# Four small reorderings in a float32 expert-mixture kernel on one core

## The chip, the cores and the metric

The kernel runs on one core of one Trainium2 chip. The metric is device time in microseconds (us). The kernel before was run three times: median 451.2 us, from 451.02 to 451.33. A profile was taken of one further execution, which took 450.84 us.

## The reference

Eight sequences of 512 tokens of width 256 attend to 64 prototypes each. The result, with the normalized token and an anchor vector, goes through a router, three experts and a gate. All in float32:

```python
nx = _layer_norm(x, ln_gamma, ln_beta)
q = nx @ Wq; k = prototype_bank @ Wk; v = prototype_bank @ Wv
weights = jax.nn.softmax(jnp.einsum('bth,bph->btp', q, k) * H ** (-0.5), axis=-1)
evidence = jnp.einsum('btp,bph->bth', weights, v)
combined = jnp.concatenate([nx, evidence, anchor], axis=-1)
router_probs = jax.nn.softmax(combined @ router_W + router_b, axis=-1)
h = jax.nn.silu(jnp.einsum('btc,ecr->bter', combined, e_w1) + e_b1)
expert_out = jnp.einsum('bter,erh->bteh', h, e_w2) + e_b2
routed = jnp.sum(expert_out * router_probs[..., None], axis=-2)
g = jax.nn.sigmoid(jax.nn.silu(combined @ gate_w1 + gate_b1) @ gate_w2 + gate_b2)
return x + g * (routed @ out_w + out_b)
```

## The kernel before

**Work.** The sequences go through in four pairs, `j` = 0 to 3; the text calls them pair 0 to pair 3, and pair 3 the last pair. Hidden dimensions lie on the 128 partitions, tokens along the free axis, 512 to a PSUM bank. The two sequences of a pair are treated as the two columns of a 2 by 2 block matrix, so that block products can be saved at the price of sums and differences of blocks, which VectorE and GpSimd make.

**Each pair has two parts.** In the first the gate's and the experts' first layers are multiplied (`gate_first`, `gate_layer`, and `expert_layer` in pair 0 or `half_layers` in the others; there the matmuls are of 64 rows, and two of them run side by side). In the second, `outputs`, come the gate's second layer and the experts' second layer, whose weights w2 have been multiplied by `out_w` beforehand. In pair 0 these are seven products of six matmuls each, with the points P1 to P7 between them; in the other pairs `twenty_products` does them as twenty block products, numbered 1 to 20.

**Twenty products.** The 512-token blocks of the pair are cut into blocks of 342 columns, `at[k, n]`. Each product is a `chain` of three matmuls, one for each expert, which appear as six records in the trace, since a float32 matmul is recorded as two. From product 19 on, the chains add in turn into two banks, Y and X. After a chain `read` lets VectorE add the bank's content to an accumulator in SBUF (`racc`), and the next chain into the same bank has to wait for that reading. Between them, differences (`less`) and sums (`plus`) of blocks of 128 x 1026 elements are made for later chains. After each chain stands a named point, c1 to c20, at which `run` calls steps of the next pair: the scores, the softmax, the transposes of its weights (`turn_weights`, parts 0, 1 and 2), the router's logits.

**Order.** The order on every engine is written out by hand: an engine issues its instructions in the order in which the code calls them, and waits at each for the semaphores of what it reads or overwrites. Which step stands at which point is set by the `put(between, point, step, ...)` lines at the end.

**What the change touches.** Four places:

- `second_layer` (line 550) multiplies w2 by `out_w` in pair 0, for one expert at a time. VectorE has transposed w2 in two halves, `k` = 0 and 1 (`transpose_second`, L548). Each bank holds two results of 256 columns, `d` = 0 and 1, and each is the sum of two matmuls, one for each `k`.
- `turn_weights`, parts 0 and 1, in pairs 1 and 2: one transpose of 128 x 512 (L850) and one of 32 x 256 (L854) on VectorE, called at point c13, ahead of product 13.
- The difference (0,1) = u - (2,0) in the last pair, called between product 16 and product 18. Product 10 multiplies it, and a sum on GpSimd reads it.
- `router_exp` of pair 1 on ScalarE, called at P3 of pair 0, ahead of `gate_first` of pair 1. `gate_first` multiplies into bank U, and a ScalarE copy (`keep_part`, L1206) saves what stands there before `gate_layer`'s product 6 is added to it.

Of the kernel before, what the change touches and what calls it, by code (L numbers as in the profile page):

```python
# [16 lines left out]
def kernel(  # L17
# [56 lines left out]
    KH = H // P  # L74
# [33 lines left out]
    def misc(name):  # L108
        spare.append(spare.pop(0))
        return bank(spare[-1], name)  # L110
# [439 lines left out]
    def second_layer(e):  # L550
        w2T = w2["T"]
        for i in range(0, RC, 2):
            ps = misc(f"ps_w2o_{e}_{i}")
            for d in range(2):
                for k in range(KH):
                    nc.tensor.matmul(  # L556
                        ps[:, d * H : (d + 1) * H], w2T[:, k, (i + d) * P : (i + d + 1) * P], ow_sb[:, k, :],
                        start=(k == 0), stop=(k == KH - 1),
                    )
            c = e * RC + i  # L560
            nc.scalar.copy(w2o[:, c : c + 2, :].rearrange("p c n -> p (c n)"), ps)
# [697 lines left out]
    def gate_first(j):  # L1259
        n = 0  # L1260
        gate_tile(j, 0, 0)
        U[n] = bank(0, f"ps_u_{j}_{n}")
        nx_product(j, n, 1, True)
        keep_part(n, 0, 0, U[n])
# [343 lines left out]
    def zero_ends(j):  # L1608
        nc.gpsimd.memset(hall[:, :, 2 * T :], 0.0)
# [13 lines left out]
    def twenty_products(j, run, gated, finish, store, last_gate):  # L1623

        last = j + 1 == NP
        V_, G = nc.vector, nc.gpsimd
# [3 lines left out]
        def less(engine, dst, p, m):  # L1630
            engine.tensor_tensor(at[dst], at[p], at[m], ALU.subtract)  # L1631

        def plus(engine, dst, p, m):
            engine.tensor_tensor(at[dst], at[p], at[m], ALU.add)  # L1634
# [71 lines left out]
            less(V_, "w", (2, 1), "u")  # L1706
        read("Y", 1, 1, ALU.subtract)
        nc.scalar.mul(at[2, 1], at[2, 0], -1.0)
        if not last:
            plus(V_, (3, 1), (0, 0), (3, 2))  # L1710
        run("c9")
        chain(20, (0, 2), 5, "X")
# [9 lines left out]
        chain(16, "w", "Y")  # L1722
        read("Y", 1, 2, ALU.subtract)
        if last:
            less(V_, (0, 1), "u", (2, 0))
            plus(G, (0, 2), (1, 0), (0, 1))
            less(G, (0, 2), (3, 0), (0, 2))
        run("c11")
# [279 lines left out]
    with tc.manual_schedule(engines=None):  # L2008
# [63 lines left out]
        for j in range(NP):  # L2072


            within, between = {}, {}

            def put(where, n, step, *args):
                where.setdefault(n, []).append(lambda: step(*args))

            if j == 0:  # L2080
                for e, points in enumerate(("AB", "SABCDE", "ACDE")):
                    for point in points:
                        put(within, (e, point), values_together, e, point)
                put(within, "gate first", value_weights, 0, 0, nc.scalar.copy, False)
                put(within, "gate early", value_differences, 0, 0)
                put(within, "gate early", value_weights, 0, 1, nc.scalar.copy, False)
                put(within, "gate", load_table, AF.Silu)
                put(within, (0, "S"), combine_x, 0, nc.vector, (3,))
                put(within, (0, "S"), value_differences, 0, 1)
                put(within, (0, "S"), router_part, 0)  # L2090
                put(within, (0, "A"), router_part, 1)
                put(within, (0, "A"), load_x, 2)
                put(within, (0, "A"), load_x, 3)
                put(within, (0, "B"), combine_weights, 1)
                put(within, (0, "B"), combine_weights, 2)
                put(within, (0, "B"), combine_gate)
                put(within, (0, "A"), router_logits, 0)
                put(within, (0, "A"), load_second, 1)
                put(within, (0, "C"), transpose_second, 0)
                put(within, (0, "C"), value_weights, 0, 2)  # L2100
                put(within, (0, "sums"), late_rows)
                put(within, (2, "W"), second_bias)
                put(within, (0, "C"), router_exp, 0)
                put(within, (0, "D"), router, 0)
                put(within, (0, "C"), load_second, 2)
                put(within, (0, "D"), second_layer, 0)
                put(within, (0, "D"), spread_probabilities, 0)
                put(within, (0, "D"), combine_second, 0)
                put(within, (1, "A"), transpose_second, 1)
                put(within, (1, "B"), second_layer, 1)  # L2110
                put(within, (1, "B"), combine_second, 1)
                put(within, (1, "C"), transpose_second, 2)
                put(within, (1, "C"), anchor_columns, 2)
                put(within, (1, "D"), second_layer, 2)
                put(within, (1, "D"), combine_second, 2)
                put(within, (1, "D"), values_together, 1, "D late")
            if j > 1:
                put(within, "gate early", router_exp, j)
                put(within, "gate early", lambda: later.pop()())
            if j == 0:  # L2120
                put(within, (2, "A"), gate_differences, 0)
            if j + 1 < NP:
                b0, b1 = 2 * j + 2, 2 * j + 3
                if j == 0:
                    put(between, "P7", load_x, b0 + 2)
                    put(between, "P7", load_x, b1 + 2)
                elif j + 2 < NP:
                    put(between, "f01", place_last_x, b1 + 2)
                if j == 0:
                    put(between, "P6", load_x_blocks, 0)  # L2130
                    put(between, "P6", load_x_blocks, 1)
                    for b in (b0, b1):
                        put(within, (0, "D"), statistics, b, 0, NT)
                    for b in (b0, b1):
                        put(within, (1, "S"), deviation, b)
                    for b in (b0, b1):
                        put(within, (1, "S"), normalize, b)
                        put(within, (1, "S"), store_x, b)
                    put(within, (1, "C"), regroup_x, b0)
                    put(within, (1, "B"), router_part, b0)  # L2140
                    put(within, (1, "B"), router_part, b1)
                put(between, "begin", transpose_blocks, b0)
                put(between, "gate", regroup_x, b1)
                put(between, "gate values" if j else "begin", value_weights, j + 1, E)
                put(between, "c2" if j else "begin", store_router_rows, j + 1)
                put(between, "c10" if j else "begin", spread_router_rows, j + 1)
                put(between, "c4" if j else "P5", transpose_blocks, b1)
                if j == NP - 3:
                    put(between, "c4", place_last_x, b0 + 2)
                put(between, "c9" if j else "P2 half", scores, j + 1)  # L2150
                if j:
                    for point, ts in (("p13", (0, 1)), ("c10", (2, 3))):
                        put(between, point, combine_x, j + 1, nc.gpsimd, ts)
                else:
                    put(between, "P2 half", combine_x, 1, nc.gpsimd)
                put(between, "c12" if j else "P7", softmax, j + 1)
                if j:
                    put(between, "c13", turn_weights, j + 1, (0, 1))
                    put(between, "c15", turn_weights, j + 1, (2,))
                    for e, point in enumerate(("c17", "c18")):  # L2160
                        put(between, point, router_logits, j + 1, (e,))
                    put(between, "c4", value_differences, j + 1, 0)
                else:
                    put(between, "P7", turn_weights, 1)
                    put(between, "P7", router_logits, 1)
                    put(between, "P7", value_differences, 1, 0)
                if not j:
                    put(between, "P3", router_exp, 1)
            if j == 0:
                for point in ("begin", "P1", "P6", "P2 half", "P2"):  # L2170
                    put(between, point, values_together, E, point)
            if not j:
                gate_first(j)
            gate_layer(j, within)
            if j:
                zero_ends(j)
                half_layers(j)
            else:
                for e in range(E):
                    expert_layer(j, e, within)  # L2180
            outputs(j, between)
# [34 lines left out]
```

## Time and profile before

| | before |
|---|---|
| median of three runs | 451.2 us (451.02 to 451.33) |
| the profiled execution | 450.84 us |
| its span, first to last instruction | 448.7 us |
| TensorE busy | 443.3 us, 99% |
| VectorE busy | 364.7 us, 81% |
| ScalarE busy | 229.4 us, 51% |
| GpSimd busy | 170.4 us, 38% |
| TensorE clock granted | 0.999 of full speed |

A line of a timeline tells when a run of like instructions began on one engine, how long it lasted, the source line, the operation, the tiles (written <- read) with buffer numbers left out, partitions x elements, how many there were, and in brackets how long the engine was idle before and what ended that. PE is TensorE, PEld its weight loads, DVE is VectorE, ACT is ScalarE, POOL is GpSimd. L1139 is the line of the helper that issues nearly all matmuls, so matmuls are told apart by their tiles. L1646 is the reading of a bank, L1631 a block difference (`less`), L1634 a block sum (`plus`). The ends of matmuls are modelled, and the bars of successive matmuls overlap.

### The profile page before, as it was taken

What the parts mean: (1) busy time and instruction counts of PE and PEld (TensorE: products, weight loads), DVE (VectorE), ACT (ScalarE), POOL (GpSimd) and SP (SyncE); (2) the same over time, 40 slices, a digit from 0 to 9 for tenths busy, and PEclk for the clock granted to TensorE, in tenths of its full rate; (3) what the DMA queues carried; (4) which work ended last, traced back from release to release, by engine and by line L of the source; (5) the groups of instructions that cost most, each with busy time, mean ns of one, the idle gap of its engine ahead of it and who ended that gap; (6) DMA issues with size and microseconds to landing.
All of it is one profiled execution on the core that took longest, in us unless ns stands there. A gap on an engine that the chain in (4) does not pass through costs nothing.

```text
span 448.7 us, 5750 instructions
## 1 busy us (share of the span) xinstructions
PE 443.3 (99%) x1807; PEld 231.7 (52%) x1807; DVE 364.7 (81%) x686; ACT 229.4 (51%) x417; POOL 170.4 (38%) x219
## 2 busy tenths in 40 slices
PE   8999999999999999999999999999999999999996
PEld 7644656444444444444666444445666444445665
DVE  3988889667969999879886989879867846689975
ACT  3545685548323257768533187668251265766000
POOL 6567767531242156109648320000465500001270
PEclk9999999999999999999999999999999999999999
DMA  8998699565741589979973294710561392000715
GB/s 251 380 188 197 108 266 166 99 106 110 76 66 23 119 187 227 162 135 114 123 120 59 39 234 106 112 30 13 81 95 29 53 223 32 1 0 10 112 20 94
DMA packets 136182, 51.20 MB, mean 114 GB/s; under 512 B 107069, under 2 KB 129529, under 8 KB 135641
## 3 DMA queue, kind: packets, MB, share of 16 engines
q1 hardware_dynamic: 113776, 29.90, 32.5%
q0 software_dynamic: 15456, 19.90, 24.6%
q10 hardware_dynamic: 6921, 1.05, 1.4%
q8 instruction: 14, 0.23, 0.2%
q14 instruction: 15, 0.12, 0.1%
HBM read 31.23 MB, written 7.39 MB: 86 GB/s over the span
## 4 chain that ended last, share of the span: by engine, by line
PE 90%; DVE 4%; DMA 2%; ACT 1%; SPq 1%; issue 0%; DVEq 0%
PE ps_u L1139 32%; PE ps_z L1139 13%; PE ps_y L1139 12%; PE ps_X L1139 6%; PE ps_Y L1139 5%; PE ps_vc L1139 3%; PE ps_gu L1139 2%; PE ps_w2o L556 2%; PE ps_V L1139 2%; PE ps_vw L930 2%; PE ps_W L1139 2%; PE ps_Z L1139 2%; DVE hall L1631 1%; PE ps_s L795 1%; PE ps_gz L1139 1%; PE ps_tokens L1139 1%
## 5 line engine op out<-in xcount | busy, mean ns | idle before, releaser
L1139 PE MATMUL ps_u<-nxT,w 64*128 64x512 f32 (+1 forms) x184 | 86.8, 592 | 0.0
L1254 DVE TENSOR_TENSOR hall<-hall,pb 128x512 f32<-128x512 f32 x96 | 62.9, 695 | 12.2 <-ACT hall L1197 12.2
L1197 ACT ACTIVATE hall<-hall,abias 128x512 f32<-128x512 f32 x72 | 49.4, 718 | 25.4 <-DVE hall L1203 25.1
L1139 PEld LDWEIGHTS ps_u<-nxT,w 64*128 64x128 f32 (+1 forms) x184 | 33.1, 187 | 26.1 <-issue 21.5
L1139 PE MATMUL ps_z<-T,ws 64*128 64x512 f32 (+1 forms) x92 | 46.4, 590 | 0.0
L1139 PE MATMUL ps_z<-nxT,ws 64*128 64x512 f32 (+1 forms) x92 | 45.9, 590 | 0.0
L1139 PE MATMUL ps_y<-nxT,w 64*128 64x512 f32 (+1 forms) x92 | 45.5, 590 | 0.0
L1139 PE MATMUL ps_u<-T,ws 64*128 64x512 f32 (+1 forms) x92 | 42.9, 590 | 0.0
L1139 PE MATMUL ps_u<-T,w 64*128 64x512 f32 (+1 forms) x98 | 42.4, 589 | 0.0
L1206 ACT COPY hall<-ps_u 128x512 f32<-128x512 f32 x48 | 27.9, 580 | 13.4 <-PE ps_u L1139 12.7
L1634 POOL TENSOR_TENSOR hall<-hall 128x1026 f32<-128x1026 f32 x5 | 14.0, 2791 | 52.0 <-DVE hall L1631 50.0
L1139 PE MATMUL ps_z<-wT,vw 64*128 64x512 f32 x56 | 27.5, 596 | 0.0
L1631 DVE TENSOR_TENSOR hall<-hall 128x1026 f32<-128x1026 f32 x21 | 26.3, 1268 | 0.4
L1139 PE MATMUL ps_z<-wT,w 64*128 64x512 f32 x48 | 24.1, 589 | 0.0
L1139 PEld LDWEIGHTS ps_z<-nxT,ws 64*128 64x128 f32 (+1 forms) x92 | 17.2, 188 | 13.3 <-issue 10.9
L1139 PEld LDWEIGHTS ps_y<-nxT,w 64*128 64x128 f32 (+1 forms) x92 | 17.3, 188 | 13.1 <-issue 13.1
L1139 PEld LDWEIGHTS ps_z<-T,ws 64*128 64x128 f32 (+1 forms) x92 | 17.3, 188 | 12.7 <-issue 11.4
L1139 PEld LDWEIGHTS ps_u<-T,ws 64*128 64x128 f32 (+1 forms) x92 | 16.1, 187 | 13.5 <-issue 11.9
L1139 PEld LDWEIGHTS ps_u<-T,w 64*128 64x128 f32 (+1 forms) x98 | 16.2, 187 | 13.2 <-issue 11.6
L1203 DVE TENSOR_TENSOR hall<-hall,ps_z 128x512 f32<-128x512 f32 x24 | 16.3, 683 | 5.9 <-PE ps_z L1139 2.8
L1197 ACT ACTIVATE hall<-ps_u,abias 128x512 f32<-128x512 f32 x24 | 16.4, 687 | 8.9 <-PE ps_u L1139 4.5
L594 POOL DMA_DIRECT2D other<-hall x1 | 1.3, 1332 | 50.1 <-ACT other L1664 50.1
(375 smaller groups left out, 1093.8 us busy)
## 6 DMA issues: line engine op xcount, KB each, us to landing
pb<-pd POOLq DMA_DIRECT2D x4, 1536.0 KB, 7.2
xb<-in_x_dram SPq DMA_DIRECT2D x64, 64.0 KB, 2.5
x<-in_x_dram SPq DMA_DIRECT2D x28, 128.0 KB, 3.7
hall<-hall POOLq DMA_DIRECT2D x6, 513.0 KB, 6.0
w<-in_L_xcond_e_w_dram SPq DMA_DIRECT2D x6, 512.0 KB, 12.6
xd<-x SPq DMA_DIRECT2D x24, 128.0 KB, 3.5
xg<-xd SPq DMA_DIRECT2D x48, 64.0 KB, 2.5
hall<-in_L_xcond_e_w_dram SPq DMA_DIRECT2D x3, 512.0 KB, 17.0
```

The source lines that it names most:

```text
L556: nc.tensor.matmul(ps[:, d * H : (d + 1) * H], w2T[:, k, (i + d) * P : (i + d + 1) * P], ow_sb[:, k, :], start=(k == 0), stop=(k == KH - 1),)
L594: nc.gpsimd.dma_start(dst, src, accum_op=ALU.add)
L795: nc.tensor.matmul(ps[side(i, h), g * NH : (g + 1) * NH], mr[:, k, 2 * j + i, g * TB : (g + 1) * TB], S["nxT", 2 * j + i][:, k, h * NH : ( ...
L930: nc.tensor.matmul(ps, vT[:, k, j * 2 * CT : (j + 1) * 2 * CT], w1[:, KH + k, n0:n1], start=(k == 0), stop=(k == KH - 1),)
L1139: return nc.tensor.matmul(ps, lhsT, rhs, start=start, stop=True, skip_group_check=not start)
L1197: nc.scalar.activation(h, h if src is None else src, AF.Silu, bias=abias[:, c, 2 * j + i : 2 * j + i + 1])
L1203: nc.vector.tensor_tensor(h, h, part, ALU.add)
L1206: nc.scalar.copy(chunk(n, i, d), part)
L1254: nc.vector.tensor_tensor(h, h, S["pb", j][:, i, :, 2 * q // RC, :], ALU.mult)
L1631: engine.tensor_tensor(at[dst], at[p], at[m], ALU.subtract)
L1634: engine.tensor_tensor(at[dst], at[p], at[m], ALU.add)
```

## The change

It moves the turning of the softmax weights from point c13 to point c14, behind the reading of product 13; makes the last pair's difference (0,1) before product 20 instead of after the reading of product 16; calls the router's exponentials of pair 1 at P4 instead of P3; and in `second_layer` swaps the loops over `d` and `k`, so that the first half of w2 is used for both results before the second. There only the first matmul of a bank opens it.

```diff
--- before.py
+++ after.py
@@ -551,11 +551,11 @@
         w2T = w2["T"]
         for i in range(0, RC, 2):
             ps = misc(f"ps_w2o_{e}_{i}")
-            for d in range(2):
-                for k in range(KH):
+            for k in range(KH):
+                for d in range(2):
                     nc.tensor.matmul(
                         ps[:, d * H : (d + 1) * H], w2T[:, k, (i + d) * P : (i + d + 1) * P], ow_sb[:, k, :],
-                        start=(k == 0), stop=(k == KH - 1),
+                        start=(k == 0 and d == 0), stop=True, skip_group_check=k + d > 0,
                     )
             c = e * RC + i
             nc.scalar.copy(w2o[:, c : c + 2, :].rearrange("p c n -> p (c n)"), ps)
@@ -1706,7 +1706,9 @@
             less(V_, "w", (2, 1), "u")
         read("Y", 1, 1, ALU.subtract)
         nc.scalar.mul(at[2, 1], at[2, 0], -1.0)
-        if not last:
+        if last:
+            less(V_, (0, 1), "u", (2, 0))
+        else:
             plus(V_, (3, 1), (0, 0), (3, 2))
         run("c9")
         chain(20, (0, 2), 5, "X")
@@ -1722,7 +1724,6 @@
         chain(16, "w", "Y")
         read("Y", 1, 2, ALU.subtract)
         if last:
-            less(V_, (0, 1), "u", (2, 0))
             plus(G, (0, 2), (1, 0), (0, 1))
             less(G, (0, 2), (3, 0), (0, 2))
         run("c11")
@@ -2155,7 +2156,7 @@
                     put(between, "P2 half", combine_x, 1, nc.gpsimd)
                 put(between, "c12" if j else "P7", softmax, j + 1)
                 if j:
-                    put(between, "c13", turn_weights, j + 1, (0, 1))
+                    put(between, "c14", turn_weights, j + 1, (0, 1))
                     put(between, "c15", turn_weights, j + 1, (2,))
                     for e, point in enumerate(("c17", "c18")):
                         put(between, point, router_logits, j + 1, (e,))
@@ -2165,7 +2166,7 @@
                     put(between, "P7", router_logits, 1)
                     put(between, "P7", value_differences, 1, 0)
                 if not j:
-                    put(between, "P3", router_exp, 1)
+                    put(between, "P4", router_exp, 1)
             if j == 0:
                 for point in ("begin", "P1", "P6", "P2 half", "P2"):
                     put(between, point, values_together, E, point)
```

**VectorE, pair 1, around products 13 and 6** (wT are the turned softmax weights, ps_X and ps_Y the two banks):

```order
 L835 RECIPROCAL rs_1825<-sm_1790 128x8
 L1646 TENSOR_TENSOR racc<-racc,ps_Y_1759 128x342
-L850 STREAM_TRANSPOSE wT_1839<-w_1784 128x512
-L854 STREAM_TRANSPOSE wT_1839<-w_1784 32x256
 L1646 TENSOR_TENSOR racc<-racc,ps_X_1801 128x342
+L850 STREAM_TRANSPOSE wT_1843<-w_1784 128x512
+L854 STREAM_TRANSPOSE wT_1843<-w_1784 32x256
 L1646 TENSOR_TENSOR racc<-racc,ps_Y_1759 128x342
-L854 STREAM_TRANSPOSE wT_1839<-w_1784 32x256 x3
+L854 STREAM_TRANSPOSE wT_1843<-w_1784 32x256 x3
 L1646 TENSOR_TENSOR racc<-racc,ps_X_1801 128x342
```

Two transposes have moved behind the reading of bank X, and stand now between it and the reading of bank Y; the other three stay where they were.

**VectorE, last pair, from the difference of product 16's block to the reading of product 18** (other is u, third the block of product 18):

```order
 L1631 TENSOR_TENSOR own<-hall,other 128x3x342
 L1646 TENSOR_TENSOR racc<-racc,ps_Y_2969 128x342
-L1646 TENSOR_TENSOR racc<-racc,ps_X_2975 128x342
+L1631 TENSOR_TENSOR hall<-other,hall 128x3x342
+L1646 TENSOR_TENSOR racc<-racc,ps_X_2976 128x342
 L1634 TENSOR_TENSOR hall<-hall,third 128x3x342
 L1646 TENSOR_TENSOR racc<-racc,ps_Y_2969 128x342
-L1631 TENSOR_TENSOR hall<-other,hall 128x3x342
-L1646 TENSOR_TENSOR racc<-racc,ps_X_2975 128x342
+L1646 TENSOR_TENSOR racc<-racc,ps_X_2976 128x342
 L1646 TENSOR_TENSOR racc<-racc,ps_Y_2969 128x342
```

The difference (0,1) has moved ahead of two readings and a sum, which now stand behind it.

**ScalarE, from pair 0 into pair 1** (ex are the router's exponentials, lg its logits, ps_u_0 the bank of `gate_first`):

```order
 L819 ACTIVATE w_1093,sm_1099<-w_1093,nmx_1100 128x2x32 x8
 L1128 ACTIVATE w_93<-w_93 128x512
-L886 ACTIVATE ex_1197<-lg_760 128x24
-L1206 COPY hg_0_1199<-ps_u_0_1200 128x512
+L1206 COPY hg_0_1197<-ps_u_0_1198 128x512
+L886 ACTIVATE ex_1216<-lg_760 128x24
 L1206 COPY hg_1_1220<-ps_z_0_1221 128x512
```

The copy of the bank and the exponentials have changed places.

## Rows read from the trace of the kernel before

**Rows 1.** The page, part 1: each engine's busy us, share of the span, instructions.

```profile
PE 443.3 (99%) x1807; PEld 231.7 (52%) x1807; DVE 364.7 (81%) x686; ACT 229.4 (51%) x417; POOL 170.4 (38%) x219
```

**Rows 2.** Waits of TensorE: us in total, times, longest us.

```profile
PE ps_X L1139 <- DVE racc L1646: 0.3, 1, 0.3
```

**Rows 3.** Timeline of TensorE, pair 1: start us, us, engine, line, operation, [idle <-releaser].

```profile
237.36 1.89 PE L1139 MATMUL ps_X<-hall,w2o 128*128 128x342 f32 x6
239.09 1.89 PE L1139 MATMUL ps_Y<-hall,w2o 128*128 128x342 f32 x6
241.32 1.99 PE L1139 MATMUL ps_X<-hall,cw 128*128 128x342 f32 x6 [0.34 <-DVE racc L1646]
```

**Rows 4.** The same view, VectorE, pair 1.

```profile
239.54 0.71 DVE L850 STREAM_TRANSPOSE wT<-w 128x512 f32<-128x512 f32 x1 [1.47 <-ACT w L840]
...
240.75 0.51 DVE L1646 TENSOR_TENSOR racc<-racc,ps_X 128x342 f32<-128x342 f32 x1
241.18 0.51 DVE L1646 TENSOR_TENSOR racc<-racc,ps_Y 128x342 f32<-128x342 f32 x1
```

**Rows 5.** The same view, TensorE, pair 2.

```profile
339.34 1.91 PE L1139 MATMUL ps_X<-hall,cw 128*128 128x342 f32 x6
```

**Rows 6.** The same view, TensorE, last pair.

```profile
423.99 1.31 PE L1139 MATMUL ps_X<-third,cw 128*128 128x342 f32 x4
...
425.89 1.99 PE L1139 MATMUL ps_Y<-hall,cw 128*128 128x342 f32 x6
```

**Rows 7.** The same view, VectorE, last pair.

```profile
422.46 0.51 DVE L1646 TENSOR_TENSOR racc<-racc,ps_X 128x342 f32<-128x342 f32 x1 [0.70 <-PE ps_X L1139]
422.89 1.22 DVE L1634 TENSOR_TENSOR hall<-hall,third 128x1026 f32<-128x1026 f32 x1
424.19 0.51 DVE L1646 TENSOR_TENSOR racc<-racc,ps_Y 128x342 f32<-128x342 f32 x1
424.62 1.22 DVE L1631 TENSOR_TENSOR hall<-other,hall 128x1026 f32<-128x1026 f32 x1
```

**Rows 8.** The same view, GpSimd, last pair.

```profile
422.80 1.25 POOL L594 DMA_DIRECT2D hall<-hall  x1 [5.36 <-ACT hall L1708]
425.99 2.36 POOL L1634 TENSOR_TENSOR hall<-hall 128x1026 f32<-128x1026 f32 x1 [1.93 <-PE ps_X L1139]
```

**Rows 9.** The same view, GpSimd and VectorE where they meet, pairs 1 and 2.

```profile
217.07 2.53 POOL L1634 TENSOR_TENSOR hall<-hall 128x1026 f32<-128x1026 f32 x1
...
218.68 2.01 DVE L1631 TENSOR_TENSOR hall<-hall 128x1026 f32<-128x1026 f32 x1
...
313.25 2.36 DVE L1631 TENSOR_TENSOR hall<-hall 128x1026 f32<-128x1026 f32 x2
...
314.65 2.83 POOL L1634 TENSOR_TENSOR hall<-hall 128x1026 f32<-128x1026 f32 x1 [50.03 <-DVE hall L1631]
```

**Rows 10.** The same view, ScalarE, end of pair 0.

```profile
152.32 0.22 ACT L886 ACTIVATE ex<-lg 128x24 f32<-128x24 f32 x1 [13.66 <-DVE lg L880]
152.45 0.57 ACT L1206 COPY hg<-ps_u 128x512 f32<-128x512 f32 x1
```

**Rows 11.** The same view, TensorE, end of pair 0.

```profile
147.09 5.31 PE L1139 MATMUL ps_u<-hall,w2o 128*128 128x512 f32 x12
152.24 1.02 PE L1139 MATMUL ps_z<-T,ws 128*128 128x512 f32 x2
153.17 1.10 PE L1139 MATMUL ps_u<-T,ws 128*128 128x512 f32 x2
```

**Rows 12.** The same view, TensorE, w2 products of the second and third expert.

```profile
65.03 3.70 PE L556 MATMUL ps_w2o<-ow_sb,hall 128*128 128x256 f32 x16
...
74.58 3.62 PE L556 MATMUL ps_w2o<-ow_sb,hall 128*128 128x256 f32 x16
```

**Rows 13.** The same view, weight loads of the second expert's w2 products.

```profile
65.44 2.89 PEld L556 LDWEIGHTS ps_w2o<-ow_sb,hall 128*128 128x128 f32 x14 [0.22 <-DVE hall L548]
```

**Rows 14.** The same view, VectorE, near the span's end.

```profile
444.93 0.29 DVE L1793 TENSOR_TENSOR y_rows<-ps_tokens,rest 84x128 f32<-84x128 f32 x1 [0.76 <-PE ps_tokens L1139]
```

## The prediction

> **What bounds the kernel now.** I read the page's busy shares first: TensorE is busy for 443.3 of the 448.7 us of the span [rows 1]. So no edit can win more than the few places where TensorE stands still, and an edit that removes none of them wins nothing. The second view, TensorE's waits, seems to say that even these are hardly there: the largest wait of a matmul for a reader of its bank is 0.3 us [rows 2]. That figure is too small. A matmul's bar runs on after its columns are in (a chain of six 342-column records lasts 1.89 us but the next one begins 1.73 us after it), so a late start hides under the bar before it. The third reading is therefore the timeline of TensorE by **starts**: take the distance from one start to the next, subtract what the same work takes where nothing is late, and add the extra length of the late bar itself, because a restarted chain is 0.10 us longer.
>
> Done over the whole span, this leaves short pauses where matmuls of full height and of half height meet, which the change does not touch, and, larger than a few hundredths of a microsecond, little else than four places that the four edits aim at. Everything else follows TensorE without a pause, so a pause removed early moves all that comes after.
>
> **The first place and its edit: turning the softmax weights (pair 1).** Regular chains start 1.73 us apart (237.36 to 239.09), but the next starts at 241.32, 2.23 us on, and is 1.99 instead of 1.89 us long [rows 3]. That is 0.50 + 0.10 = **0.60 us lost**. This chain (number 9) adds into the bank X that the chain of 237.36 filled, so it must wait until VectorE has read X. That chain's bar ended at 239.25, but VectorE stood waiting for ScalarE's last softmax multiplication, then turned the weights (239.54 to 240.75, two transposes, 1.21 us), and only then read X, at 240.75 [rows 4]. TensorE starts 0.06 us after that reading ends.
>
> The edit puts the two transposes behind the reading. X is then read at 239.27 to 239.78, and chain 9 can start on its regular beat, 239.09 + 1.73 = 240.82. Behind it the transposes run from about 239.8 to 241.0. What is late next? The reading of bank Y stands behind them; Y's chain ends at 239.09 + 1.89 = 240.98, so this reading also starts at about 241.0, where it stood at 241.18, and ends at 241.5. Chain 5, the next into Y, needs that at 240.82 + 1.73 = 242.55: 1.0 us to spare. The turned weights are not used before the next pair. No instruction is added, no DMA moves, no queue but VectorE's is passed. Gain 0.60. The same edit in pair 2 finds nothing to win: there the chain behind the same transposes starts on its beat and is 1.91 us long [rows 5], so I count 0.
>
> **The second place: the last pair's block difference.** Here the chain at 425.89 starts 1.90 us after the one before it instead of 1.73 and lasts 1.99 us [rows 6]: 0.17 + 0.10 = **0.27 us lost**. It multiplies the block (0,1), and VectorE finishes that difference only at 425.84: it begins at 424.62, behind two readings and a sum [rows 7]. VectorE had been idle for 0.70 us ahead of 422.46 [rows 7]. The edit lets the difference start there, at about 421.76; it takes 1.22 us, to 422.98. The reading of X behind it slips from 422.46 to about 422.9 and ends at 423.4, before the chain at 423.99 wants that bank. The sum slips to 423.35 to 424.6, the reading of Y to about 424.5 to 425.0; the chain that waited wants Y and the block at 423.99 + 1.73 = 425.72. All are there, with 0.7 us to spare. Gain 0.27.
>
> One more engine is moved by this: GpSimd's sum of the same block waits for the difference. It issued a DMA from 422.80 to 424.05, stood idle 1.93 us and began at 425.99 [rows 8]; now it can begin at 424.05, under VectorE's sum. The trace shows what such a meeting costs: while GpSimd's sum ran from 217.07 to 219.60, VectorE's difference of the usual 1.22 us took 2.01 us and ended 1.09 us after GpSimd did. In the other order, with VectorE's two differences begun at 313.25 and GpSimd's sum issued under the second, GpSimd's took 2.83 us instead of the 2.36 of [rows 8], and VectorE's two kept 2.36 together [rows 9]. The Trainium skill (SBUF — State Buffer, section Who interferes with whom) states this as a lock: a VectorE instruction with two SBUF inputs and a GpSimd instruction that reads SBUF exclude each other, and the one that starts first keeps the port for its whole length. The trace agrees, by the 2.01 us. VectorE's sum starts at 423.35, 0.7 us ahead of GpSimd's, so as in the second of these meetings it is GpSimd that waits, and its result is multiplied only several chains later. I count 0; the other order is a rival below, with its price. By the rule, too, nothing is added unless GpSimd is first.
>
> **The third place: the router's exponentials (into pair 1).** Six 512-column matmuls take 5.15 us from 147.09 to 152.24, so one takes 0.86; the second product after them starts 0.93 us after the first and lasts 1.10 instead of 1.02 us [rows 11]: 0.07 + 0.08 = **0.15 us lost**. It adds into the bank of the gate's first product, and must wait for ScalarE's copy of it. That product stands ahead of 147.09, but the copy was issued behind the exponentials, for which ScalarE stood idle 13.66 us until the logits came at 152.3; the copy ran from 152.45 to 153.02 [rows 10]. With the copy first it runs at about 147.3 and the exponentials start at 152.32 as before, so their reader sees nothing. Gain 0.15.
>
> **The fourth place: w2 products.** A block of sixteen records (two banks) lasts 3.62 us for the third expert and 3.70 for the second [rows 12]. The extra **0.08 us** is a weight load that waited for VectorE's transpose of w2's second half [rows 13]; it was wanted by the second matmul, and in the new order only by the third, 0.43 us later. Gain 0.08. In the other two experts no such wait shows, and the number of matmuls (24), their sizes and the copies are the same: 0. Taking the two halves of a bank in turn has no row of its own in the trace. Its price lies between nothing and a restart for each bank, 6 x 0.10 = 0.6 with the 0.10 of [rows 3]. I take nothing: the sixteen records already change the half or the bank three times, and they follow each other at the rate of the twelve records of twice the width, which start 5.15 / 12 = 0.43 us apart [rows 11] (16 x 0.215 = 3.43 from start to start, and the bar's run-on). For the same reason a gain beyond the wait is excluded. I keep 0.2 of that 0.6 for the range.
>
> **The sum.** 0.60 + 0.27 + 0.15 + 0.08 = 1.10 us. The profiled execution took 450.84 us (span 448.7 and 2.1 around it) and becomes 449.7. It is 0.36 below the median of the runs, 451.2; by that, **450.1**. What a measurement of this kernel can tell from no change is about 0.2%, 0.9 us, so 450.3 is the bound of faster, and the forecast lies just beyond it.
>
> **The rivals.**
> - *The first gain comes back as another wait.* The order of pair 1 gives VectorE two transposes between two readings. If ScalarE's weights came 1.0 us later than at 239.5, chain 5 would stop for Y as chain 9 does now. Or VectorE, which goes from pair 1 into pair 2 with hardly a gap, follows 0.6 us later than its feeder and stops a product there. For it: VectorE is busy 81% of the span [rows 1]. Against it: it stood idle ahead of the readings and products in [rows 4, 7, 14], so it has gaps to catch up in. The time is then 451.2 - 0.50 = 450.7, within the bound.
> - *The end does not follow.* The gains reach the end only if the last stores hang on TensorE. They do: VectorE stood idle 0.76 us for the last products before the last multiplication [rows 14]. If the last place's 0.27 were lost for all that, 450.4, also within.
> - *GpSimd gets in first (slower).* If VectorE's sum of the last pair should start after 424.05, 0.7 us later than I reckon, GpSimd's sum holds it until 424.05 + 2.36 = 426.4 [rows 8]; the sum then ends at 427.5 by the 1.09 of [rows 9], Y is read by 428.0, and the chain starts 2.3 us after its beat. Then the last place costs 2.4 in place of 0.27: 451.2 - 0.83 + 2.1 = 452.5. Against it: the idle 0.70 us [rows 7] gives the difference its start, and nothing of it waits for a DMA that the earlier difference did not already need.
>
> **How the numbers follow.** All four waits go: 0.74, at 449.8 to 450.3; a part of that (0.06) measures above 450.3. One of the first two gains is lost, or the alternating halves cost: 0.20, at 450.4 to 450.7, a little of it (0.01) reading as faster. GpSimd's case and anything like it: 0.06, of which 0.01 within the bound. So faster 0.69, same 0.26, slower 0.05. The range takes in the first two cases, and the spread of the runs (0.3): 449.6 to 450.9.
>
> **What would show it.** In the changed profile: the chain after the reading of X in pair 1 starts 1.73 us after its forerunner and lasts 1.89; the last pair's chain behind the block difference likewise, with VectorE's difference at about 421.8 less the shift; ScalarE's copy at about 147.2 and no 1.10 us bar; the second expert's sixteen records in 3.62 us. GpSimd's sum in the last pair should start about 1.9 us earlier, lengthened. I am wrong if a new distance above 1.73 stands one or two chains behind the removed ones, above all at chain 5 of pair 1, or if VectorE's sum in the last pair is 2 us long or more.

## The result, and the profile after

The changed kernel takes **453.69 us** (median of 6 runs, 452.52 to 454.74), the kernel before, measured beside it, 451.25 (451.02 to 451.69): ratio **1.0052, 95% interval 1.0036 to 1.0069**. It is slower by 2.4 us where I forecast 1.1 us faster. The profiled execution took 454.06 us; its span is 451.9 us, against 448.7.

**The four waits are gone.** TensorE's timeline of the changed kernel, at the places of [rows 12], [rows 11] and [rows 3] (start us, us, engine, line, operation, tiles):

```profile
64.91 3.61 PE L556 MATMUL ps_w2o<-ow_sb,hall 128*128 128x256 f32 x16
...
152.03 1.02 PE L1139 MATMUL ps_z<-T,ws 128*128 128x512 f32 x2
152.89 1.02 PE L1139 MATMUL ps_u<-T,ws 128*128 128x512 f32 x2
...
237.01 1.89 PE L1139 MATMUL ps_X<-hall,w2o 128*128 128x342 f32 x6
238.74 1.89 PE L1139 MATMUL ps_Y<-hall,w2o 128*128 128x342 f32 x6
240.46 1.89 PE L1139 MATMUL ps_X<-hall,cw 128*128 128x342 f32 x6
```

The second expert's sixteen records last 3.61 instead of 3.70 us. The two router products follow in 0.86, without the 1.10 us bar. Chain 9 starts 1.72 us after its forerunner instead of 2.23. Against the kernel before, pair 2 begins 254.33 instead of 255.29, 0.96 earlier: 0.83 from these three places (0.08, 0.15, 0.60) and 0.13 from the loads at the very start.

**The last pair loses all of it and more.** The same view there, VectorE as in [rows 7], GpSimd as in [rows 8], TensorE as in [rows 6]:

```profile
421.03 1.22 DVE L1631 TENSOR_TENSOR hall<-other,hall 128x1026 f32<-128x1026 f32 x1
422.17 0.51 DVE L1646 TENSOR_TENSOR racc<-racc,ps_X 128x342 f32<-128x342 f32 x1
422.59 4.32 DVE L1634 TENSOR_TENSOR hall<-hall,third 128x1026 f32<-128x1026 f32 x1
426.83 0.50 DVE L1646 TENSOR_TENSOR racc<-racc,ps_Y 128x342 f32<-128x342 f32 x1
...
422.16 1.25 POOL L594 DMA_DIRECT2D hall<-hall  x1 [5.36 <-ACT hall L1708]
422.96 2.85 POOL L1634 TENSOR_TENSOR hall<-hall 128x1026 f32<-128x1026 f32 x1
425.89 2.88 POOL L1631 TENSOR_TENSOR hall<-hall 128x1026 f32<-128x1026 f32 x1
...
423.35 1.32 PE L1139 MATMUL ps_X<-third,cw 128*128 128x342 f32 x4
424.50 0.74 PE L1139 MATMUL ps_X<-third,cw_rest 128*128 128x342 f32 x2
427.38 3.65 PE L1139 MATMUL ps_Y<-hall,cw 128*128 128x342 f32 x6 [2.15 <-DVE racc L1646]
430.83 1.39 PE L1139 MATMUL ps_X<-hall,w2o 128*128 128x342 f32 x4
```

The difference (0,1) now begins at 421.03, as meant. But VectorE's sum (1,1) behind it takes 4.32 us instead of 1.22. GpSimd's sum begins 0.37 us after it, and VectorE's ends 1.10 us after GpSimd's (422.59 + 4.32 = 426.91, 422.96 + 2.85 = 425.81): by its length it did nothing until GpSimd was through. The reading of Y comes late, and chain 10, whose beat is 423.35 + 1.73 = 425.08, starts at 427.38, **2.30 us late**. In the list of TensorE's waits it is now the longest:

```profile
PE ps_Y L1139 <- DVE racc L1646: 2.1, 1, 2.1
```

Behind that pause the six records last 3.65 us instead of 1.89. The busy time by stretches shows why (stretch, its us, busy us of PE, PEld, DVE, ACT, POOL, then the granted clock, and the DMA engines' share and GB/s):

```profile
400.00:424.00 24.00, 24.00 (x81) 13.95 (x78) 23.27 (x29) 11.01 (x16) 4.45 (x4) 1.00 0.28 45
424.00:427.00 3.00, 1.24 (x5) 0.49 (x3) 3.00 (x2) 0.00 (x0) 2.92 (x2) 1.00 1.09 175
427.00:428.00 1.00, 0.62 (x2) 0.39 (x3) 0.84 (x2) 0.00 (x0) 1.00 (x1) 0.78 0.00 0
428.00:431.00 3.00, 3.00 (x7) 1.82 (x6) 0.00 (x0) 0.00 (x0) 0.77 (x1) 0.50 0.00 0
431.00:440.00 9.00, 9.00 (x36) 6.02 (x35) 7.64 (x13) 0.00 (x0) 3.49 (x4) 1.00 0.00 0
```

TensorE stood idle from 424.50 + 0.74 = 425.24 to 427.38, at its full clock (2.4 GHz), and was granted half (1.2 GHz) from 428 to 431, soon after it had begun again; with the 0.78 of the microsecond before, some 3.4 us in all.

**A smaller loss** lies in pair 2. TensorE is 0.96 us ahead at its begin but 0.64 at the last pair's product 18 (423.35 against the 423.99 of [rows 6]); 0.32 go back in half products that wait for VectorE. Then 2.13 us go from product 18 to chain 10 (0.64 ahead there, then 427.38 - 425.89 = 1.49 behind), and 1.7 more with the clock: 1.49 + 1.7 = the 3.2 us by which the span grew.

### The profile page after: what moved, and what is told of

It is laid out like the page before. It is cut to its first block, busy times and chain, and to the rows that moved or that the text cites. A ratio compares the mean times of both kernels' runs of the same rounds, so it can differ in the third digit from the quotient of the medians.

```text
span 451.9 us, 5750 instructions
## 1 busy us (share of the span) xinstructions
PE 444.9 (98%) x1807; PEld 240.5 (53%) x1807; DVE 368.6 (82%) x686; ACT 229.4 (51%) x417; POOL 171.6 (38%) x219
## 4 chain that ended last, share of the span: by engine, by line
PE 96%; DVE 2%; DMA 1%; SPq 0%; issue 0%; DVEq 0%
PE ps_u L1139 31%; PE ps_z L1139 13%; PE ps_y L1139 12%; PE ps_Y L1139 7%; PE ps_X L1139 6%; PE ps_gu L1139 3%; PE ps_V L1139 3%; PE ps_vc L1139 3%; PE ps_Z L1139 3%; PE ps_w2o L556 2%; PE ps_W L1139 2%; PE ps_vw L930 2%; PE ps_s L795 2%; PE ps_gz L1139 2%; DVE hall L1634 1%; PE ps_tokens L1139 1%
## 5 line engine op out<-in xcount | busy, mean ns | idle before, releaser
L1203 DVE TENSOR_TENSOR hall<-hall,ps_z 128x512 f32<-128x512 f32 x24 | 16.3, 683 | 5.8 <-PE ps_z L1139 2.9
```

Of the source, the lines that this page charges most:

```text
L1203: nc.vector.tensor_tensor(h, h, part, ALU.add)
```

## The experiments

Theory: GpSimd's sum (0,2), set free by the moved difference, holds VectorE's sum (1,1); chain 10 waits and the clock falls. Rivals: the loss comes from the other edits, or VectorE waits for a transfer.

### Where the loss comes from

**Only the last pair's edit, on the kernel before.**

```diff
-        if not last:
+        if last:
+            less(V_, (0, 1), "u", (2, 0))
+        else:
             plus(V_, (3, 1), (0, 0), (3, 2))
...
-            less(V_, (0, 1), "u", (2, 0))
             plus(G, (0, 2), (1, 0), (0, 1))
```

> The kernel before with the last pair's difference (0,1) moved alone. Theory (the meeting): GpSimd's sum of the same block, set free earlier, meets VectorE's sum of block (1,1) and holds it until its own end; chain 10 starts 2.1 to 2.4 us late, and the clock falls behind that pause as in the changed kernel, 1.7 us more: about 451.2 + 2.1 + 1.7 = 455, 453.4 if the clock does not fall; VectorE's sum takes 4.0 to 4.4 us. Rival (one of the other three edits brings the loss, the last pair's wait only falls where it does because all runs 1 us earlier): VectorE's sum takes 1.22 us and the time is 451.0 (0.27 won).

Measured: 454.43 us (452.91 to 455.50), ratio 1.0059 (1.0042 to 1.0077). VectorE's sum takes 4.32 us, TensorE waits 2.15. This edit alone brings the whole loss. The two sums:

```profile
424.18 4.32 DVE L1634 TENSOR_TENSOR hall<-hall,third 128x1026 f32<-128x1026 f32 x1
...
424.55 2.85 POOL L1634 TENSOR_TENSOR hall<-hall 128x1026 f32<-128x1026 f32 x1
```

**The change without that edit** (the same lines back).

> The changed kernel with the last pair's difference put back behind the reading of product 16; the other three edits stay. Theory (the meeting): no meeting in the last pair, the three gains of 0.83 us less the 0.33 that pair 2 gives back: 451.25 - 0.50 = 450.7, VectorE's sum 1.22 us, chain 10 0.17 late as before. Rival (the loss comes from the other edits): about 453 or more, with chain 10 late all the same.

Measured: 451.19 us, ratio 0.9997 (0.9989 to 1.0006); the sum takes 1.22 us. The other edits do not bring the loss, but of their 0.83 us only 0.13 shows (-0.27 to 0.50).

### What holds VectorE's sum

**Sum and difference change places on VectorE.**

```diff
         if last:
-            less(V_, (0, 1), "u", (2, 0))
+            plus(V_, (1, 1), (1, 1), "v")
...
         if last:
-            plus(V_, (1, 1), (1, 1), "v")
+            less(V_, (0, 1), "u", (2, 0))
```

> The changed kernel, where VectorE makes the last pair's sum (1,1) at the place where the change put the difference (0,1), and this difference behind the reading of X, where the sum stood: the two change places, the work is the same. GpSimd's sum waits for the difference, so it can begin only behind both. Theory (the meeting): VectorE's sum and difference take 1.22 us each, chain 10 is on its beat, the 0.27 is won and the clock stays at 1.0: 451.25 - 1.10 + 0.33 = 450.5. Rival (the sum waits for the landing of a transfer that reads or writes the same tile, not for GpSimd's sum): the sum is long at its new place as well and the chain late, 452 or more.

Measured: 450.73 us, ratio 0.9991 (0.9981 to 1.0000). Both take 1.22 us, chain 10 starts on its beat (423.81 + 1.73 = 425.54) and lasts 1.89. One of the twelve runs took 453.04 us at full clock; it has no trace, and why stays open.

**GpSimd's sum on VectorE.**

```diff
-            plus(G, (0, 2), (1, 0), (0, 1))
+            plus(V_, (0, 2), (1, 0), (0, 1))
```

> The changed kernel with GpSimd's sum (0,2) = (1,0) + (0,1) made by VectorE instead, behind the reading of Y; the transfer that GpSimd issues just ahead of it and GpSimd's difference behind it stay. Theory (the meeting with GpSimd's sum): VectorE's sum (1,1) takes 1.22 us, chain 10 is on its beat: 450.5. Rival (GpSimd's issuing of the transfer, or the transfer itself, holds VectorE): the sum (1,1) is still some 3 to 4 us long and the time 453 or more.

Measured: **450.04 us, ratio 0.9973 (0.9962 to 0.9984)**, the lowest median of this study. VectorE's and GpSimd's timelines in the last pair:

```profile
423.29 1.22 DVE L1634 TENSOR_TENSOR hall<-hall,third 128x1026 f32<-128x1026 f32 x1
424.43 0.51 DVE L1646 TENSOR_TENSOR racc<-racc,ps_Y 128x342 f32<-128x342 f32 x1
424.85 1.22 DVE L1634 TENSOR_TENSOR hall<-hall 128x1026 f32<-128x1026 f32 x1
...
422.87 1.25 POOL L594 DMA_DIRECT2D hall<-hall  x1 [5.37 <-ACT hall L1708]
```

The sum begins in the middle of GpSimd's issuing bar, as before, and takes 1.22 us. So neither the issue nor the transfer holds VectorE; GpSimd's sum does.

### Which of the two keeps the port

The port, in the prediction's word, is what VectorE's sum and GpSimd's cannot hold at the same time. Three kinds of edits shift the two sums against each other in the changed kernel. **Memsets ahead of the sum**: three of 128x128, eight of them, one of 128x8, one of 128x128, into a tile of their own (its line is left out).

```diff
+            G.memset(pause[:, :128], 0.0)
             plus(G, (0, 2), (1, 0), (0, 1))
```

> The changed kernel with three memsets of a 128x128 tile of their own on GpSimd between its transfer's issue and its sum (0,2): GpSimd's sum starts some 0.4 to 0.6 us later, VectorE's sum (1,1) leads by 0.8 to 1.0 us instead of 0.37. Theory 1 (the one that asks first keeps the port, and GpSimd's asks some time ahead of what its bar shows): VectorE's sum takes 1.22 us, GpSimd's waits, chain 10 is on its beat: 450.5. Theory 2 (GpSimd's sum wins the port however late it comes): VectorE's sum is 4.5 us or more, chain 10 later still, 454 to 455.

> The same with eight memsets: GpSimd's sum starts 1.0 to 1.6 us later, when VectorE's sum has run for all of its 1.22 us or nearly. Theory 1: VectorE's sum takes 1.22 us, 450.5. Theory 2: at the edge, VectorE's sum either 1.22 us or over 4 us. If the memsets themselves held VectorE, its sum would be about 1 us longer and the chain 10 on its beat or 0.5 late.

> The changed kernel with a single memset of 128x8 on GpSimd ahead of its sum (0,2). By the bars of the run with three memsets (the first took 0.70 us, 0.5 more than the others, and began 0.77 us after the transfer's issue), GpSimd's sum would begin some 0.9 to 1.1 us behind VectorE's, while VectorE's still runs. Theory 1 (who asks first keeps the port): VectorE's sum 1.22 us, GpSimd's bar longer than 2.36, 450.7. Theory 2 (GpSimd takes the port from a sum that has begun): VectorE's sum 4 us or more, 453 to 455.

> The changed kernel with one memset of 128x128 on GpSimd ahead of its sum. In the run with three, the second began 1.52 us after the transfer's issue; GpSimd's sum should begin about there, 1.0 to 1.1 us behind VectorE's sum, which comes behind a reading of a bank and is still under way. If the lead decides: VectorE's sum 1.22 us, GpSimd's bar over 2.36, 450.7. If what stands ahead of VectorE's sum decides (behind a reading of a bank it loses, behind another sum or difference it keeps): 4 us or more, 453.3 to 455.

Measured: 450.74 (0.9986, 0.9977 to 0.9995), 450.67 (0.9980, 0.9969 to 0.9991), 454.87 (1.0078, 1.0062 to 1.0093), 454.89 us (1.0069, 1.0044 to 1.0093), the last two of four runs each. With three and eight memsets GpSimd's sum begins only when VectorE's is done, so these runs confirm the price but not who wins. One memset did not delay it as I expected: its bar lies over the memset's. VectorE then lost with leads of 0.41 and 0.51 us. The latter, with one of 128x128:

```profile
422.84 0.50 DVE L1646 TENSOR_TENSOR racc<-racc,ps_X 128x342 f32<-128x342 f32 x1
423.26 4.45 DVE L1634 TENSOR_TENSOR hall<-hall,third 128x1026 f32<-128x1026 f32 x1
...
423.60 0.70 POOL L1728 MEMSET pause<- 128x128 f32 x1
423.77 2.85 POOL L1634 TENSOR_TENSOR hall<-hall 128x1026 f32<-128x1026 f32 x1
```

**The transfer's issue behind GpSimd's two operations.**

```diff
-        accumulated(at[2, 1], at[2, 2])
+        if not last:
+            accumulated(at[2, 1], at[2, 2])
...
             less(G, (0, 2), (3, 0), (0, 2))
+            accumulated(at[2, 1], at[2, 2])
```

> The changed kernel with GpSimd's issue of the transfer (2,1) += (2,2) behind its sum and difference instead of ahead of them. Theory 1: GpSimd's sum starts right behind VectorE's difference (0,1), clearly ahead of VectorE's sum, and holds that for less long: VectorE's sum ends 1.1 us after GpSimd's, takes 3.2 to 3.7 us, chain 10 is 1.3 to 1.7 us late: 452.0, 453.7 if the clock falls behind this shorter pause too. Rival (it is the issue of the transfer that lets GpSimd in or holds VectorE): VectorE's sum 1.22 us, 450.6.

Measured: 451.97 us, ratio 1.0014 (1.0004 to 1.0025). GpSimd's sum is first by 0.17 us; VectorE's takes 3.27 and ends 1.08 after it:

```profile
424.39 3.27 DVE L1634 TENSOR_TENSOR hall<-hall,third 128x1026 f32<-128x1026 f32 x1
...
424.22 2.36 POOL L1634 TENSOR_TENSOR hall<-hall 128x1026 f32<-128x1026 f32 x1 [5.60 <-DVE hall L1631]
```

Chain 10 is 1.26 us late, and in none of the ten runs was the mean clock below 0.998: this shorter pause did not bring the clock down.

**VectorE's difference and sum back to back**, the reading of X behind both; and the same with the transfer's issue behind.

```diff
             less(V_, (0, 1), "u", (2, 0))
+            plus(V_, (1, 1), (1, 1), "v")
...
         if last:
-            plus(V_, (1, 1), (1, 1), "v")
+            pass
```

> The changed kernel where VectorE's sum (1,1) follows its difference (0,1) at once and the reading of X comes behind both. VectorE's sum then starts some 0.4 us ahead of where it stood, 0.8 ahead of GpSimd's bar, and with no reading of a bank between the two. Theory 1: VectorE's sum takes 1.22 us, GpSimd's waits; the reading of X is late by 0.5 for product 18, nothing else: 450.6 + 0.5 = 451.1. Theory 2: the sum takes 4 us or more, product 18 is 3.5 us late, 454 or more.

> VectorE's difference and sum back to back, and GpSimd's issue of the transfer behind its sum: GpSimd's sum waits for VectorE's difference alone and begins some 0.2 us behind VectorE's sum, a shorter lead than the 0.37 and 0.41 us with which VectorE's sum lost behind a reading of a bank. If the lead decides: VectorE's sum takes 3 us or more, the readings of X and Y and products 18 and 10 come 2 us late or more: 453 or more. If what stands ahead decides: VectorE's sum 1.22 us, GpSimd's waits, product 18 is late by 0.5 to 0.6: 451.1.

Measured: 451.17 (0.9992, 0.9981 to 1.0004) and 451.39 us (0.9996, 0.9986 to 1.0006), product 18 late by 0.5 in both. VectorE keeps the port, in the second with a lead of only 0.24 us:

```profile
422.00 1.22 DVE L1631 TENSOR_TENSOR hall<-other,hall 128x1026 f32<-128x1026 f32 x1
423.13 1.22 DVE L1634 TENSOR_TENSOR hall<-hall,third 128x1026 f32<-128x1026 f32 x1
...
423.37 3.20 POOL L1634 TENSOR_TENSOR hall<-hall 128x1026 f32<-128x1026 f32 x1 [5.61 <-DVE hall L1631]
```

GpSimd's bar ends 2.22 us after VectorE's sum, about its own 2.36. So the lead of the bars does not decide here. In the last pair VectorE kept the port behind a difference of two SBUF blocks with 0.24 and 0.80 us, and lost it behind a reading of a bank (L1646) with 0.37 to 0.51.

What stands ahead on VectorE does not decide by itself either. In the run with the 128x8 memset, at the begin of the kernel, VectorE's L786 came behind a reading of a bank too (L1203) and kept the port with a lead of 0.10 us; GpSimd's L269, 0.72 us in other runs, took 1.17:

```profile
32.74 0.69 DVE L1203 TENSOR_TENSOR hg<-hg,ps_w 128x512 f32<-128x512 f32 x1 [0.45 <-PE ps_w L1139]
33.34 0.69 DVE L786 TENSOR_TENSOR T<-nxT,T 128x512 f32<-128x512 f32 x1
...
33.44 1.17 POOL L269 TENSOR_TENSOR w<-w 128x256 f32<-128x256 f32 x1
```

And in pair 1 of the run with the transfer's issue behind, VectorE's product, behind a reading of a bank (L1646), waited for two operations of GpSimd: one that had begun before it, and a second whose bar began 0.56 us after its own:

```profile
244.03 2.42 DVE L1913 TENSOR_TENSOR racc<-racc,hg 128x512 f32<-128x512 f32 x1
...
243.36 1.30 POOL L786 TENSOR_TENSOR nxT<-nxT 128x512 f32<-128x512 f32 x1
244.59 1.29 POOL L786 TENSOR_TENSOR T<-nxT,T 128x512 f32<-128x512 f32 x1
```

Why VectorE lost in the last pair, and how long a lead would be enough there, stays open.

### Why the first three gains hardly show

**The turning alone, on the kernel before** (c13 to c14).

```diff
-                    put(between, "c13", turn_weights, j + 1, (0, 1))
+                    put(between, "c14", turn_weights, j + 1, (0, 1))
```

> The kernel before with the turning of the softmax weights moved alone. My theory of the small give-back: behind the turning, VectorE's L1911 multiplication of pair 1 meets a multiplication of GpSimd (L786) and ends 0.55 us after it; GpSimd's own chain of work does not start earlier by the 0.60, so VectorE enters pair 2 up to 0.9 us behind TensorE, and pair 2's half products lose what VectorE is late beyond about 0.1: of the 0.60 some 0.2 to 0.4 is left, 450.9 to 451.1. Rival (the prediction's step): all 0.60 reaches the end, 450.7, and no late start stands in pair 2.

Measured: 451.50 us, ratio 1.0000 (0.9991 to 1.0009): of 0.60 us nothing shows, and at most 0.4 can be left. In the changed kernel's pair 1, VectorE (L1911), and GpSimd:

```profile
243.00 1.64 DVE L1911 TENSOR_TENSOR racc<-racc,hg 128x512 f32<-128x512 f32 x1
...
246.26 1.02 DVE L866 TENSOR_TENSOR pv<-w,vr 128x512 f32<-128x512 f32 x1
...
242.79 1.29 POOL L786 TENSOR_TENSOR T<-nxT,T 128x512 f32<-128x512 f32 x1
245.47 1.27 POOL L1921 TENSOR_TENSOR hg<-hg,xb 128x512 f32<-128x512 f32 x1 [1.38 <-DVE hg L1919]
```

Both of VectorE's bars, 0.7 us elsewhere, end 0.55 us after GpSimd's. GpSimd works without a gap from 230.82 and gains nothing from a turn at 240, so VectorE is held that much longer. This shows as lateness into pair 2: VectorE's first L1203 there less the start of TensorE's ps_y<-wT,vw. Before, and in the changed kernel:

```profile
255.29 0.69 PE L1139 MATMUL ps_y<-wT,vw 64*128 64x512 f32 x1
255.43 0.66 DVE L1203 TENSOR_TENSOR hg<-hg,ps_u 128x512 f32<-128x512 f32 x1
...
254.33 0.69 PE L1139 MATMUL ps_y<-wT,vw 64*128 64x512 f32 x1
254.80 0.65 DVE L1203 TENSOR_TENSOR hg<-hg,ps_u 128x512 f32<-128x512 f32 x1
```

The table sets this lateness beside TensorE's time from there to pair 3's first gate product (ps_gu<-hg,gw_sb), and beside the end of GpSimd's last L786 of pair 1, counted from the start of TensorE's product 20; all in us, read from the timelines:

| kernel | GpSimd's L786 ends, after product 20 begins | VectorE late | TensorE, pair 2 to pair 3's gate |
|---|---|---|---|
| before | 13.86 | 0.13 | 147.06 |
| before, turning alone | 14.14 | 0.53 | 147.50 |
| changed | 14.08 | 0.47 | 147.38 |
| changed, sum first | 13.71 | 0.14 | 147.04 |
| changed, eight memsets | 14.41 | 0.80 | 147.94 |
| changed, sum on VectorE, turning back | 14.42 | 0.21 | 147.24 |

What VectorE is late beyond some 0.1 us TensorE pays in pair 2: in 15 of the 16 profiles TensorE's time is 147.0 us and that lateness, to within 0.25. GpSimd's place differs by some tenths from one profile to the next, also between kernels that do the same work up to there (why, I did not test), and at the same place (14.41, 14.42) the kernel with the turning moved pays 0.70 more: the 0.60 comes back.

**GpSimd's last difference of tokens later**, on the kernel with the sum on VectorE.

```diff
-                    for point, ts in (("p13", (0, 1)), ("c10", (2, 3))):
+                    for point, ts in (("p13", (0, 1)), ("c10", (2,)), ("c18", (3,))):
```

> The changed kernel with GpSimd's sum (0,2) of the last pair on VectorE (as in the run of that), and the last of GpSimd's four differences of tokens (L786) in pairs 1 and 2 called at c18 instead of c10, so that it runs behind GpSimd's first residual addition and no longer under VectorE's L1911. Theory of the give-back: L1911 takes 0.7 us, VectorE enters pair 2 0.15 us behind TensorE, no late starts stand in pair 2: all four gains are kept, 451.3 - 1.10 = 450.2 or less, with a smaller spread. Rival (the give-back has another cause): pair 2 loses 0.3 to 0.9 all the same, and the time is that of the run without this move, 450.0 to 450.5.

Measured: 450.94 us, ratio 0.9990 (0.9981 to 0.9999); a miss. L1911 takes 0.83 us, but GpSimd's difference now meets L866, which takes 1.45; VectorE is 0.89 late and TensorE's stretch takes 148.43. The meeting had only moved. This is the sixteenth profile: by its lateness the stretch should take 147.8. Against the run with the sum on VectorE, 0.3 of the excess arises some 8 us into pair 3, into which the same difference was moved.

**The sum on VectorE, the turning back at c13.**

> The changed kernel with GpSimd's sum (0,2) of the last pair on VectorE, and the turning of the weights back at c13. It tells what the turning is worth in a kernel without the meeting in the last pair. Theory of the give-back: without the turning's gain the time is 451.35 - 0.27 - 0.15 - 0.08 = 450.85, against 450.04 measured and 450.2 to 450.6 to be expected with it. If the turning were worth its whole 0.60, with the mean give-back of a kernel without it at nothing: 450.85 against 450.25.

Measured: 450.40 us, ratio 0.9977 (0.9968 to 0.9985), beside 0.9973 with the turning moved: no difference that can be told. Its gain of 1.0 us (0.7 to 1.4) exceeds the 0.50 that the remaining edits account for. One profile of the kernel before cannot say how often that kernel pays in pair 2 itself; with only the last pair's edit, which cannot reach back there, it was 0.44 late and took 147.48. So the rest is open.

## Why the prediction was wrong

- **The four terms were right where I took them.** The w2 products, the router's exponentials and chain 9 of pair 1 run on the beat; chain 10 of the last pair does as soon as the two sums no longer meet (sum and difference changed places).
- **The step that failed** is "now it can begin at 424.05" with "VectorE's sum starts at 423.35, 0.7 us ahead of GpSimd's, so ... it is GpSimd that waits". I put the meeting at 0; it made chain 10 2.30 us late, and the clock took 1.7 more. Two things were wrong. I took GpSimd's sum to start at the end of its issuing bar of 1.25 us. It starts 0.80 us after that bar's begin (422.16, 422.96), over it. The trace of the kernel before shows the same ahead of GpSimd's sum of 217.07 in [rows 9], and I passed over it:

```profile
216.28 1.28 POOL L594 DMA_DIRECT2D w2o<-w2o  x1 [1.37 <-ACT w2o L630]
```

This alone would not have turned my forecast: 422.80 + 0.80 = 423.60 is still 0.25 us behind VectorE's 423.35, and in the second meeting of [rows 9] GpSimd's sum came 0.26 us behind VectorE's second difference (313.25 + 2.36 - 1.22 = 314.39, then 314.65) and waited. What failed is the choice of that meeting as the model for who waits. There VectorE's two differences stood back to back; here its sum followed a reading of a bank, had a lead of 0.37, and lost. The Trainium skill (SBUF — State Buffer, section Who interferes with whom) says that issue order decides who blocks. These bars do not agree: VectorE's, first by 0.37 us, lost. Whether GpSimd asked for the port before its bar begins, no trace here shows.
- **The rival had the right mechanism, by a condition that did not come true.** GpSimd's sum held VectorE's, though VectorE's bar did not start after it. It gave the last place 2.4 us, the chain 2.3 late; measured 2.30. That the two agree so well is luck: set 0.64 us later, as TensorE stood before the change, GpSimd's sum began at 423.60 instead of 424.05 and took 2.85 us instead of 2.36. The rival's time, 452.5, lacked the clock: of 20 runs of the four kernels with the long sum (this one, its edit alone, the two single memsets), 12 had a mean clock of 0.996 and took 454.06 to 455.71 us, the other 8 took 452.52 to 453.72. I gave it 0.06 because I took the lead of the bars to decide.
- **The range was too narrow at the top** for a second reason: "the first gain comes back as another wait", VectorE's lateness into pair 2, came true too. I set against it that VectorE has gaps; behind chain 9 it has no use of them, since GpSimd sets its pace.

## What to carry to other kernels

Before an operation is freed on one engine, look what stands beside it on the engine that shares its port, and price the order that you don't want. A GpSimd operation may begin before the issuing bar ahead of it ends, and a lead of a few tenths of a microsecond by the bars is not to be built on: 0.37 to 0.51 us lost here, 0.24 kept. A gain on TensorE counts only as far as the engines that feed the next stage gain it too.

## What the runs showed of the hardware that I had not expected

- VectorE's sum of two SBUF blocks, begun 0.37 to 0.51 us ahead of GpSimd's, behind a reading of a bank, waited for all of GpSimd's: 4.3 to 4.5 us instead of 1.22.
- GpSimd's bars overlap: a sum over an issue by 0.45 us, over a memset by 0.53. The first could be read before the change (216.28 + 1.28 = 217.56 against 217.07).
- A pause of TensorE of 2.15 us was followed by 3.4 us at half clock; one of 2.18, in the profile with the 128x8 memset, by none (granted clock 1.00 throughout). Of the 20 runs with the long sum, 12 had the lower mean clock. A pause of 1.09 us (a chain 1.26 late) was followed by none in ten runs.
